# A graph layer with linear attention and an expert network: the flag's work among the first edge groups, chunks of 5 and 3 node tiles, the experts' first products in another bank ring

## The chip, the cores and the metric

The kernel runs on one core of a Trainium2 chip as one launch. The metric is the device time of that launch in microseconds (us), lower is better. In this text PE is TensorE, PEld its weight loads, DVE VectorE, ACT ScalarE, POOL GpSimd and SP SyncE; the last issues DMAs.

## The reference

There are 6250 nodes of 256 features and 106250 edges, sorted by their destination, with 64 edge features each. All numbers are float32.

```python
xn = _layernorm(x)
# graph part: one message per edge, summed over the edges of a destination
msgs = silu(concat([xn[src], edge_attr], -1) @ W + b)
gnn  = layernorm(segment_sum(msgs, dst, 6250)) * gamma + beta
# linear attention over all nodes, 8 heads of 64
q, k, v = split(xn @ Wqkv.T);  k, v = inst_norm(k), inst_norm(v)   # per head
mix  = (q @ (k.T @ v) / 6250) @ Wout.T + bout
x = x + gnn + mix
# expert part: each node goes to one of 32 experts (256 -> 64 -> 256)
xf  = _layernorm(x);  idx = argmax(xf @ router_w.T + router_b)
out = relu(relu(xf @ W1[idx] + b1[idx]) @ W2[idx] + b2[idx])
x = x + out
```

## The kernel before

**Tiles.** The nodes are 49 tiles of 128 (the last is partial). The edges are 208 groups of 512; a group is gathered in four pieces of 128 edges, 831 gathers in all.

**Stage one** (`stage_one`) runs to the first gather. For a pair j of node tiles it normalizes (ACT), transposes on PE (`turn`, L353), multiplies by the node part of the weight on PE (`project`, L363), adds the bias on DVE and stores to `proj` in DRAM. Statistics of the layer norm (DVE; `shift` and `inv`) are dealt out over the pairs. Between pairs, `columns` (L372 to L379) transposes a table of integers held as floats: `src` behind pair 3, right behind its cast on POOL (L394); the places of destinations, `rel`, at pair 10, after POOL's work on `dst` at pair 6; and first columns of `dst` at the end. From these a chain on DVE (to L456) makes `row_of`. Last comes the flag, one number that says whether the fast selection is valid for these edges: an iota `g_i` on POOL, a chain of `bounds` on DVE (from L460), four reductions over 128x896 numbers (L465, L473), a sum over rows by PE (`pflag`, L482) and a copy to `unlike`.

**Edge loop** (from L1562, `for g in range(NG)`). The order of instructions on each engine is that of the program. One turn g issues, in this order: the gathers of group g+3 on POOL (L1432; the tile `gat` has 6 buffers), four products `h` on PE (L1571), the add of `h` and `gat` on DVE (L1573), a selection matrix `s1` on DVE (L1579), the transpose of the edge features of group g+1 (PE L1448, ACT copy L1452), the silu on ACT (L1589), the load of edge features four groups ahead on ACT's DMA queue (L1417), and `work.step`, which lets a planner add other work. Every second turn follows `level2` (PE `sum`, L1553) and `level1` (PE `po`, L1526, ACT copy L1535), which sum the messages of two groups by selection matrices. `po` is the last reader of a `gat` buffer.

**The planner.** `work.step` gives 2.7 us of PE and 3.8 us of DVE a turn to generators in a fixed order, each of which states what its step costs. They are: `attention()` (load and turn the weights, L497 to L523; then batches of two node tiles: `kv`, L540 to L570; then the matrix); `finish()` with one `chunk` per entry of `CHUNKS`; `clears()` (SP stores of zeros); and the expert work. `chunk` mixes, takes moments (DVE), makes `inv2`, normalizes into `wide`, transposes on PE (`pt`, L784, ACT copy `xfT`, L786), makes the router's products (`lg`, L772) for two tiles at a time, then picks the expert (`hot`), and ranks tokens by expert (`prank`, L839, DVE chain with `logit`, L851). The tokens of a round are then sent to rows sorted by expert in DRAM (`send`, POOL, L1051) and read back in blocks by SP (`xb`, L1066), whose weights follow on SP's queue (L1168, L1171, L1217). The first round takes 28 tiles.

**Experts.** `layers` works on quads of blocks: transposes (`pt`, L1088, DVE copy L1094), first products `phid` (L1100), relu on ACT (`hid`, L1110), second products `py` (L1124, L1135), relu on ACT into `xb` (L1144), a store (L1146). Accumulator memory is handed out in rings by tag: "h" one buffer of two banks, "t", "sum" and "kv" two banks each. `phid`, `py`, `kv`, `lg` and `prank` share "kv"; `po` and all transposes share "t". After the last edge group the rest of the work drains ("draining", "late"), and `collect` and `dense` finish the nodes.

Of the kernel before, what the change touches and what calls it, by code (L numbers as in the profile page):

```python
# [8 lines left out]
F32 = mybir.dt.float32  # L9
# [6 lines left out]
PSUM = bass.MemoryType.PSUM  # L16
# [12 lines left out]
GE = P * KE  # L29
KS = 2  # L30
SPAN = P // (KE * KS)
CHUNKS = (6, 6, 6, 5, 5, 5, 5, 4, 3, 2, 2)
CH = max(CHUNKS)
FIRST = (2, 4, 6, 10, 13, 14)
AB = 2
KV = 4
HB = 64
BB = 2
# [24 lines left out]
def kernel(  # L63
# [187 lines left out]
    mix = const.tile([P, DC, D], F32, name="mix")  # L251


    def stage_one(early, pre_ps):
        def bank(tag, shape, name, bufs=2):
            return pre_ps.tile(shape, F32, tag=tag, name=name, bufs=bufs)

# [130 lines left out]
        for j in range(NP + 1):  # L388
            if j < NP:
                turn(j)  # L390
            if j + 1 < NP:
                normalize(j + 1)
            if j == 3:
                nc.gpsimd.tensor_copy(src_f, src_r)  # L394
                columns(lambda b: src_f[:, b, :], src_T)
            if j == 6:
                nc.gpsimd.tensor_copy(dst_f, dst_r)
                nc.gpsimd.tensor_sub(rel, dst_f, dst_f[:, :, 0:1].to_broadcast([P, EB, P]))
            if j == 10:
                columns(lambda b: rel[:, b, :], rel_T)  # L400
            if j >= 1:
                pp = project(j - 1)
            if j >= 1:
                add(j - 1, pp)
            go_on(j)
# [48 lines left out]
                row_of[q, :], row_of[q, :], h_f[q, :], by_sum[q, 0, k, :], op0=ALU.mult, op1=ALU.add  # L454
            )
        nc.vector.scalar_tensor_tensor(row_of, row_of, r_f, starts, op0=ALU.add, op1=ALU.subtract)  # L456

        g_i = early.tile([P, EB], I32, name="g_i")
        nc.gpsimd.iota(g_i, pattern=[[P, EB]], base=0, channel_multiplier=1)
        nc.vector.tensor_scalar(g_i, g_i, (KE * KS).bit_length() - 1, None, op0=ALU.logical_shift_right)  # L460
        g_f = early.tile([P, EB], F32, name="g_f")
        nc.vector.tensor_copy(g_f, g_i)
        low, high = bounds(g_f, [P, EB], "tb")
        bad = early.tile([P, EB], F32, name="bad")
        nc.vector.tensor_reduce(bad, rel, axis=AX.X, op=ALU.max)  # L465
        nc.vector.tensor_scalar(bad, bad, float(SPAN), None, op0=ALU.is_ge)
        for source, op, limit, test in (
            (rel, ALU.min, None, ALU.is_lt),
            (dst_f, ALU.max, high, ALU.is_ge),
            (dst_f, ALU.min, low, ALU.is_lt),  # L470
        ):
            some = early.tile([P, EB], F32, name="some", bufs=2)
            nc.vector.tensor_reduce(some, source, axis=AX.X, op=op)  # L473
            if limit is None:
                nc.vector.tensor_scalar(some, some, 0.0, None, op0=test)
            else:
                nc.vector.tensor_tensor(some, some, limit, op=test)
            nc.vector.tensor_add(bad, bad, some)
        bad1 = early.tile([P, 1], F32, name="bad1")
        nc.vector.tensor_reduce(bad1, bad, axis=AX.X, op=ALU.add)  # L480
        pb = bank("o", [1, 1], "pflag", 3)
        nc.tensor.matmul(pb, bad1, ones[:, 0:1], start=True, stop=True)  # L482
        nc.vector.tensor_copy(unlike, pb)

# [131 lines left out]
    class Nodes:  # L616
# [114 lines left out]
        def chunk(self, t0, t1):  # L731
# [4 lines left out]
            def behind(stage):  # L736
                return before is None or self.at[before] >= stage
# [11 lines left out]
                moments(mv2, t - t0, X[:, t, :])  # L749
                yield pe, dve + 0.6, int(t == t1 - 1)  # L750
            self.at[t0] = 1
            while not behind(2):
                yield 0.0, 0.0, 1
            inv2 = inv_std(mv2, m, LN_EPS, "l2")
            on_act = self.in_order and self.work.draining
            if on_act:
# [2 lines left out]
                    shift[:, :m], mv2[:, :m, 0], -1.0, inv2[:, :m], op0=ALU.mult, op1=ALU.mult  # L759
                )  # L760
            yield 0.0, 1.9, 1
            logit = self.pool.tile([P, CH, NE], F32, name="logit", bufs=2)
            pairs = [list(range(t, min(t + 2, t1))) for t in range(t0, t1, 2)]
            turned = {}
            for i in range(len(pairs) + 2):
                pe = dve = 0.0
                if i >= 2:
                    lg = self.bank("kv", [P, 2, NE], "lg")
                    for k, t in enumerate(pairs[i - 2]):
                        xfT = turned.pop(t)  # L770
                        for c in range(DC):
                            nc.tensor.matmul(  # L772
                                lg[:, k, :], xfT[:, c, :], rw_t[:, c, :], start=(c == 0), stop=(c == DC - 1)
                            )
                    n, q = len(pairs[i - 2]), pairs[i - 2][0] - t0
                    nc.vector.tensor_add(
                        logit[:, q : q + n, :], lg[:, :n, :], rb[:, None, :].to_broadcast([P, n, NE])
                    )
                    pe, dve = pe + 0.5, dve + 0.3
                if 1 <= i <= len(pairs):  # L780
                    for t in pairs[i - 1]:
                        pt = self.bank("t", [P, DC, P], "pt")
                        for c in range(DC):
                            nc.tensor.transpose(pt[:, c, :], wide[:, t, c * P : (c + 1) * P], ident)  # L784
                        turned[t] = self.pool.tile([P, DC, P], F32, name="xfT", bufs=2)
                        nc.scalar.copy(turned[t], pt)  # L786
                    pe += 0.5
                if i < len(pairs):
                    for t in pairs[i]:
                        k = t - t0  # L790
                        if on_act:
                            nc.scalar.activation(
                                wide[:, t, :],
                                X[:, t, :],
                                AF.Identity,
                                bias=shift[:, k : k + 1],
                                scale=inv2[:, k : k + 1],
                            )
                            continue
                        nc.vector.tensor_scalar(  # L800
                            wide[:, t, :],
                            X[:, t, :],
                            mv2[:, k, 0:1],
                            inv2[:, k : k + 1],
                            op0=ALU.subtract,
                            op1=ALU.mult,
                        )
                        dve += 0.4
                yield pe, dve, 1
# [268 lines left out]
        def layers(self, pool, r, b0, xb, w1_of, w2_of, b1_of, one_of):  # L1078
# [14 lines left out]
            else:  # L1093
                nc.vector.tensor_copy(xbT, pt)  # L1094
            yield 0.6, 0.0 if late else 0.7, 1, 1.0
            ph = self.bank("kv", [P, QB // BB, HB], "phid")
            for j in pairs:
                for c in range(DC):
                    for i in range(BB):
# [284 lines left out]
    def ordered(arm):  # L1384
        with ExitStack() as edge_scope:
# [6 lines left out]
            ]  # L1392
            nodes = Nodes(node, rounds, True)
            work = nodes.work
            with tc.tile_pool(name="early", bufs=1) as early, tc.tile_pool(name="pre_ps", bufs=2, space=PSUM) as pre_ps:
                stage_one(early, pre_ps)
            psum = arm.enter_context(tc.tile_pool(name="psum", bufs=2, space=PSUM))

            def bank(tag, shape, name, bufs=2):
                return psum.tile(shape, F32, tag=tag, name=name, bufs=bufs)  # L1400

            nodes.bank = bank
            nodes.load_biases()
            opens = {t: min(g for g in range(NQ) if window(g)[0] <= t <= window(g)[1]) for t in range(NT)}
            closes = {t: max(g for g in range(NQ) if window(g)[0] <= t <= window(g)[1]) for t in range(NT)}
# [60 lines left out]
                closed.append((t0, t1))  # L1466

            attn_scope = ExitStack()
            attn = attn_scope.enter_context(tc.tile_pool(name="attn", bufs=1))
            moe_scope = ExitStack()  # L1470
            closed = []

            def attention():
                w = {}
                yield from weights(attn, bank, w)
                batches = []
# [345 lines left out]
```

## Time and profile before

| | |
|---|---|
| four runs | 1360.34, 1362.83, 1364.42, 1365.96 us; median 1363.62 |
| profiled execution | 1361.14 us, span 1359.3, mean granted clock 0.918 |
| busy | PE 1120.7 us (82%), DVE 823.3 (61%), ACT 564.5 (42%), POOL 943.7 (69%) |
| gathers | first 85.30, last 1236.86 us; 831 of 965 ns |
| DMA | 227.60 MB, mean 167 GB/s |

A row of a timeline reads: start in us, duration, engine, line, operation, out<-in, how many, and in brackets the idle time of that engine before it with what ended it. Instructions of one kind in a row are drawn together. "issue" means that the engine waited for nothing that the profile shows. The wait table gives the waiting instruction, what it waited for, the sum in us, how often, and the longest.

### The profile page before, as it was taken

The numbers are of one execution on the slowest core, as the hardware profiler recorded it, in microseconds if no ns is written. First come the engines' busy times: TensorE is split into PE (matmuls) and PEld (weight loads), VectorE is DVE, ScalarE is ACT, GpSimd is POOL, SyncE is SP. The second block draws the span as 40 slices with busy tenths as digits, with TensorE's granted clock in tenths as the row PEclk, the third lists the DMA queues.
The fourth block names the chain that finished last, engine by engine and source line by source line (L and its number), as shares of the span: only waits on it lengthen the run. The fifth ranks groups of instructions, "written<-read, shape, count | busy, mean of one in ns | idle before, by whom it ended". The sixth has DMA issues, their size and how long they took to land. (4 is left out here: it accounts for less than half of the span.)

```text
span 1359.3 us, 24393 instructions
## 1 busy us (share of the span) xinstructions
PE 1120.7 (82%) x8301; PEld 671.9 (49%) x8301; DVE 823.3 (61%) x2107; ACT 564.5 (42%) x1046; POOL 943.7 (69%) x1046
## 2 busy tenths in 40 slices
PE   5948999988888998878978886648878888987796
PEld 4834545444444544445654554325545555553453
DVE  7864767766666777567886777424545555554621
ACT  3725555544545554433333332113434444342342
POOL 3656777777777777777777777775775577573671
PEclk8977999999999999989998998667889999997698
DMA  8349544444444454584444445557887688562494
GB/s 264 116 128 373 142 130 133 132 128 129 132 127 131 130 133 127 144 261 133 129 132 130 127 132 152 166 162 207 237 236 220 193 234 231 172 194 70 143 307 131
DMA packets 243794, 227.60 MB, mean 167 GB/s; under 512 B 130920, under 2 KB 213836, under 8 KB 243660
## 3 DMA queue, kind: packets, MB, share of 16 engines
q0 software_dynamic: 44384, 121.18, 30.6%
q1 hardware_dynamic: 91096, 77.41, 17.8%
q10 hardware_dynamic: 108180, 27.34, 8.9%
q8 instruction: 69, 1.13, 0.3%
q14 instruction: 65, 0.53, 0.1%
HBM read 180.14 MB, written 45.70 MB: 166 GB/s over the span
## 5 line engine op out<-in xcount | busy, mean ns | idle before, releaser
L1432 POOL DMA_INDIRECT gat<-proj,src_T x831 | 802.0, 965 | 304.2 <-issue 246.9
L1573 DVE TENSOR_TENSOR gat<-h,gat 128x1024 f32<-128x1024 f32 x208 | 254.2, 1222 | 270.7 <-PE h L1571 138.3
L1589 ACT ACTIVATE gat<-gat 128x1024 f32<-128x1024 f32 x208 | 219.9, 1057 | 226.2 <-DVE gat L1573 209.4
L1571 PE MATMUL h<-ge,eT 64*128 64x256 f32 x1664 | 249.2, 420 | 44.7 <-DVE gat L1573 43.5
L1571 PEld LDWEIGHTS h<-ge,eT 64*128 64x128 f32 x1664 | 154.6, 196 | 136.0 <-issue 65.7
L1553 PE MATMUL sum<-part,s 128*128 128x256 f32 x400 | 124.0, 436 | 71.5 <-DVE s L1542 70.7
L540 PE MATMUL kv<-kv_w,wide 128*128 128x512 f32 x392 | 180.2, 602 | 2.2 <-DVE kv_w L518 2.2
L1452 ACT COPY eT<-pt 128x256 f32<-128x256 f32 x208 | 77.0, 370 | 201.2 <-PE pt L1448 191.6
L1553 PEld LDWEIGHTS sum<-part,s 128*128 128x128 f32 x400 | 76.4, 211 | 109.0 <-DVE s L1542 95.6
L1526 PE MATMUL po<-gat,s 128*32 128x256 f32 x1664 | 122.9, 417 | 0.0
L1535 ACT COPY part<-po 128x256 f32<-128x256 f32 x104 | 38.7, 372 | 195.2 <-PE po L1526 178.1
L540 PEld LDWEIGHTS kv<-kv_w,wide 128*128 128x128 f32 x392 | 71.8, 194 | 73.8 <-issue 70.4
L1448 PE MATMUL pt<-ident,ea 128*128 128x128 f32 x416 | 92.9, 306 | 5.1 <-ACT xfT L786 4.7
L547 DVE TENSOR_REDUCE var<-sq 128x16 f32<-128x1024 f32 x49 | 59.7, 1219 | 52.9 <-ACT sq L546 52.9
L1448 PEld LDWEIGHTS pt<-ident,ea 128*128 128x128 f32 x416 | 42.5, 143 | 77.2 <-issue 68.8
L1526 PEld LDWEIGHTS po<-gat,s 128*32 128x32 f32 x1664 | 46.0, 116 | 61.0 <-issue 35.1
L1051 POOL DMA_INDIRECT xso<-wide,slot x47 | 47.3, 1005 | 36.4 <-DVE slot L965 26.4
L1094 DVE COPY xbT<-pt 128x512 f32<-128x512 f32 x39 | 26.8, 687 | 64.0 <-PE pt L1088 63.9
L1579 DVE TENSOR_TENSOR s<-rel_T,ramp 128x128 f32<-128x128 f32 x208 | 58.9, 283 | 0.0
L720 PE MATMUL pres<-mix,wide 128*128 128x256 f32 x196 | 53.3, 408 | 5.1 <-DVE X L721 3.5
L543 ACT COPY kv<-kv 128x512 f32<-128x512 f32 x98 | 53.0, 577 | 3.5 <-PE kv L540 2.9
L347 POOL TENSOR_TENSOR X<-X,bo 128x256 f32<-128x256 f32 x49 | 34.7, 729 | 27.3 <-ACT xn L344 23.0
(298 smaller groups left out, 1426.9 us busy)
## 6 DMA issues: line engine op xcount, KB each, us to landing
ea<-in_edge_attr_dram ACTq DMA_DIRECT2D x203, 128.0 KB
gat<-proj,src_T POOLq DMA_INDIRECT x831
xso<-zero SPq DMA_DIRECT2D x51, 256.0 KB
xb<-xso SPq DMA_DIRECT2D x51, 256.0 KB
yso<-xb SPq DMA_DIRECT2D x51, 256.0 KB
proj<-pr SPq DMA_DIRECT2D x24, 256.0 KB
out_dram<-X SPq DMA_DIRECT2D x22, 256.0 KB
w1t<-in_L_ffn_W_dram SPq DMA_DIRECT2D x76, 64.0 KB
```

What stands on the lines that cost most here:

```text
L540: nc.tensor.matmul(b, xnT(t0 + j, c), kv_w[:, c, s * F : (s + 1) * F], start=(c == 0), stop=(c == DC - 1))
L547: nc.vector.tensor_reduce(var[:, j * 2 * HEADS : (j + 1) * 2 * HEADS], sq, axis=AX.X, op=ALU.add)
L720: nc.tensor.matmul(p, xnT(t, c), mix[:, c, :], start=(c == 0), stop=(c == DC - 1))
L1432: nc.gpsimd.indirect_dma_start(out=gat[:n, k % 2, k // 2, :], out_offset=None, in_=proj[:], in_offset=bass.IndirectOffsetOnAxis(ap=src_T[: ...
L1448: nc.tensor.transpose(pt[:, j, :], ea[:, 2 * j : 2 * j + 2, :].rearrange("p k d -> p (k d)"), ident)
L1452: nc.scalar.copy(eT, pt)
L1526: nc.tensor.matmul(po[k * wide_k : (k + 1) * wide_k, :], s1[:, k, :], msg[:, k % 2, k // 2, :], start=(g == here[0]), stop=(g == here[-1]) ...
L1553: nc.tensor.matmul(sums[t], s2[:, (t - lo) * P : (t - lo + 1) * P], part, start=(q == opens[t]), stop=(q == closes[t]),)
L1571: nc.tensor.matmul(h[:, s, j, :], eTs[g][half, j, :], ge[half, :], start=True, stop=True)
L1573: nc.vector.tensor_add(gats[g], h, gats[g])
L1579: nc.vector.tensor_tensor(s1s[g], rel_T[:, at, None].to_broadcast([P, KE, SPAN * KS]), ramp[:, None, r0 : r0 + SPAN * KS].to_broadcast([P, ...
L1589: nc.scalar.activation(gats[g], gats[g], AF.Silu)
```

## The change

It has five parts. (1) `CHUNKS` becomes twelve entries of at most 5, the first round now 5, 5, 5, 5, 5, 3. (2) Up to three tiles (`TG`) go through the router's transposes and products at a time. (3) A chunk may take `inv2` once the chunk before is past its own, and waits for it only afterwards. (4) In stage one the src columns go from pair 3 to 7 with their cast at 4, the dst work from 6 to 9, the rel columns from 10 to 13; and `stage_one` becomes a generator that ends at `row_of`, whose rest, the flag, is handed out by `attention()` in steps of 3.8 us of DVE, ahead of the attention's weights; the tiles of stage one are released only then, and those of the attention opened after that. (5) `phid` takes its accumulator from "t" instead of "kv", except while draining.

```diff
@@ -29,9 +29,10 @@
 GE = P * KE
 KS = 2
 SPAN = P // (KE * KS)
-CHUNKS = (6, 6, 6, 5, 5, 5, 5, 4, 3, 2, 2)
+CHUNKS = (5, 5, 5, 5, 5, 3, 5, 5, 4, 3, 2, 2)
 CH = max(CHUNKS)
 FIRST = (2, 4, 6, 10, 13, 14)
+TG = 3
 AB = 2
 KV = 4
 HB = 64
@@ -251,7 +252,9 @@
     mix = const.tile([P, DC, D], F32, name="mix")
 
 
-    def stage_one(early, pre_ps):
+    def stage_one(early, pre_ps, later_bank):
+
+
         def bank(tag, shape, name, bufs=2):
             return pre_ps.tile(shape, F32, tag=tag, name=name, bufs=bufs)
 
@@ -390,13 +393,14 @@
                 turn(j)
             if j + 1 < NP:
                 normalize(j + 1)
-            if j == 3:
+            if j == 4:
                 nc.gpsimd.tensor_copy(src_f, src_r)
+            if j == 7:
                 columns(lambda b: src_f[:, b, :], src_T)
-            if j == 6:
+            if j == 9:
                 nc.gpsimd.tensor_copy(dst_f, dst_r)
                 nc.gpsimd.tensor_sub(rel, dst_f, dst_f[:, :, 0:1].to_broadcast([P, EB, P]))
-            if j == 10:
+            if j == 13:
                 columns(lambda b: rel[:, b, :], rel_T)
             if j >= 1:
                 pp = project(j - 1)
@@ -454,13 +458,14 @@
                 row_of[q, :], row_of[q, :], h_f[q, :], by_sum[q, 0, k, :], op0=ALU.mult, op1=ALU.add
             )
         nc.vector.scalar_tensor_tensor(row_of, row_of, r_f, starts, op0=ALU.add, op1=ALU.subtract)
-
+        yield
         g_i = early.tile([P, EB], I32, name="g_i")
         nc.gpsimd.iota(g_i, pattern=[[P, EB]], base=0, channel_multiplier=1)
         nc.vector.tensor_scalar(g_i, g_i, (KE * KS).bit_length() - 1, None, op0=ALU.logical_shift_right)
         g_f = early.tile([P, EB], F32, name="g_f")
         nc.vector.tensor_copy(g_f, g_i)
         low, high = bounds(g_f, [P, EB], "tb")
+        yield
         bad = early.tile([P, EB], F32, name="bad")
         nc.vector.tensor_reduce(bad, rel, axis=AX.X, op=ALU.max)
         nc.vector.tensor_scalar(bad, bad, float(SPAN), None, op0=ALU.is_ge)
@@ -469,6 +474,8 @@
             (dst_f, ALU.max, high, ALU.is_ge),
             (dst_f, ALU.min, low, ALU.is_lt),
         ):
+            if limit is high:
+                yield
             some = early.tile([P, EB], F32, name="some", bufs=2)
             nc.vector.tensor_reduce(some, source, axis=AX.X, op=op)
             if limit is None:
@@ -478,7 +485,8 @@
             nc.vector.tensor_add(bad, bad, some)
         bad1 = early.tile([P, 1], F32, name="bad1")
         nc.vector.tensor_reduce(bad1, bad, axis=AX.X, op=ALU.add)
-        pb = bank("o", [1, 1], "pflag", 3)
+        yield
+        pb = later_bank("kv", [1, 1], "pflag")
         nc.tensor.matmul(pb, bad1, ones[:, 0:1], start=True, stop=True)
         nc.vector.tensor_copy(unlike, pb)
 
@@ -749,7 +757,7 @@
                 moments(mv2, t - t0, X[:, t, :])
                 yield pe, dve + 0.6, int(t == t1 - 1)
             self.at[t0] = 1
-            while not behind(2):
+            while not behind(1.5):
                 yield 0.0, 0.0, 1
             inv2 = inv_std(mv2, m, LN_EPS, "l2")
             on_act = self.in_order and self.work.draining
@@ -759,13 +767,18 @@
                     shift[:, :m], mv2[:, :m, 0], -1.0, inv2[:, :m], op0=ALU.mult, op1=ALU.mult
                 )
             yield 0.0, 1.9, 1
+            while not behind(2):
+                yield 0.0, 0.0, 1
+            self.at[t0] = 1.5
             logit = self.pool.tile([P, CH, NE], F32, name="logit", bufs=2)
-            pairs = [list(range(t, min(t + 2, t1))) for t in range(t0, t1, 2)]
+            parts = -(-m // TG)
+            cuts = [t0 + m * i // parts for i in range(parts + 1)]
+            pairs = [list(range(a, b)) for a, b in zip(cuts, cuts[1:])]
             turned = {}
             for i in range(len(pairs) + 2):
                 pe = dve = 0.0
                 if i >= 2:
-                    lg = self.bank("kv", [P, 2, NE], "lg")
+                    lg = self.bank("kv", [P, TG, NE], "lg")
                     for k, t in enumerate(pairs[i - 2]):
                         xfT = turned.pop(t)
                         for c in range(DC):
@@ -776,15 +789,15 @@
                     nc.vector.tensor_add(
                         logit[:, q : q + n, :], lg[:, :n, :], rb[:, None, :].to_broadcast([P, n, NE])
                     )
-                    pe, dve = pe + 0.5, dve + 0.3
+                    pe, dve = pe + 0.25 * n, dve + 0.3
                 if 1 <= i <= len(pairs):
                     for t in pairs[i - 1]:
                         pt = self.bank("t", [P, DC, P], "pt")
                         for c in range(DC):
                             nc.tensor.transpose(pt[:, c, :], wide[:, t, c * P : (c + 1) * P], ident)
-                        turned[t] = self.pool.tile([P, DC, P], F32, name="xfT", bufs=2)
+                        turned[t] = self.pool.tile([P, DC, P], F32, name="xfT", bufs=TG)
                         nc.scalar.copy(turned[t], pt)
-                    pe += 0.5
+                        pe += 0.25
                 if i < len(pairs):
                     for t in pairs[i]:
                         k = t - t0
@@ -1093,7 +1106,8 @@
             else:
                 nc.vector.tensor_copy(xbT, pt)
             yield 0.6, 0.0 if late else 0.7, 1, 1.0
-            ph = self.bank("kv", [P, QB // BB, HB], "phid")
+
+            ph = self.bank("kv" if late else "t", [P, QB // BB, HB], "phid")
             for j in pairs:
                 for c in range(DC):
                     for i in range(BB):
@@ -1392,14 +1406,17 @@
             ]
             nodes = Nodes(node, rounds, True)
             work = nodes.work
-            with tc.tile_pool(name="early", bufs=1) as early, tc.tile_pool(name="pre_ps", bufs=2, space=PSUM) as pre_ps:
-                stage_one(early, pre_ps)
-            psum = arm.enter_context(tc.tile_pool(name="psum", bufs=2, space=PSUM))
 
             def bank(tag, shape, name, bufs=2):
                 return psum.tile(shape, F32, tag=tag, name=name, bufs=bufs)
 
             nodes.bank = bank
+            early_scope = ExitStack()
+            early = early_scope.enter_context(tc.tile_pool(name="early", bufs=1))
+            with tc.tile_pool(name="pre_ps", bufs=2, space=PSUM) as pre_ps:
+                first_stage = stage_one(early, pre_ps, bank)
+                next(first_stage)
+            psum = arm.enter_context(tc.tile_pool(name="psum", bufs=2, space=PSUM))
             nodes.load_biases()
             opens = {t: min(g for g in range(NQ) if window(g)[0] <= t <= window(g)[1]) for t in range(NT)}
             closes = {t: max(g for g in range(NQ) if window(g)[0] <= t <= window(g)[1]) for t in range(NT)}
@@ -1466,11 +1483,14 @@
                 closed.append((t0, t1))
 
             attn_scope = ExitStack()
-            attn = attn_scope.enter_context(tc.tile_pool(name="attn", bufs=1))
             moe_scope = ExitStack()
             closed = []
 
             def attention():
+                for _ in first_stage:
+                    yield 0.0, 3.8, 0
+                early_scope.close()
+                attn = attn_scope.enter_context(tc.tile_pool(name="attn", bufs=1))
                 w = {}
                 yield from weights(attn, bank, w)
                 batches = []
```

## The prediction

> **What bounds the kernel now.** The busy row first, then the costliest groups.
>
> ```profile
> PE 1120.7 (82%) x8301; PEld 671.9 (49%) x8301; DVE 823.3 (61%) x2107; ACT 564.5 (42%) x1046; POOL 943.7 (69%) x1046
> ...
> L1432 POOL DMA_INDIRECT gat<-proj,src_T x831 | 802.0, 965 | 304.2 <-issue 246.9
> ```
>
> PE is busiest, but most of the span is paced by POOL. POOL's timeline has gathers back to back from 85.30 to 1237.85 us, one each 0.953 + 0.30 = 1.257 us, 5.03 us a group; 831 make 1044.6 of those 1152.6 us. So the loop can lose time only where a gather starts late, and gain only there or at its two ends. These are the first two late places, and two of a long series:
>
> ```profile
> 85.30 1.14 POOL L1432 DMA_INDIRECT gat<-proj,src_T  x1 [8.30 <-DMA b_sb<-in_L_ffn_b_dram]
> ...
> 122.42 0.95 POOL L1432 DMA_INDIRECT gat<-proj,src_T  x1 [6.24 <-ACT kv L543]
> ...
> 925.68 0.95 POOL L1432 DMA_INDIRECT gat<-proj,src_T  x1 [4.47 <-issue]
> ...
> 1010.12 0.95 POOL L1432 DMA_INDIRECT gat<-proj,src_T  x1 [2.43 <-issue]
> ```
>
> The bracket is the idle time before. Between 123 and 925 us no gather is late at all. Net of the usual 0.30, the gathers at 925.68, 936.23 and 950.77 lose 8.8 us, and eleven between 1008 and 1184 lose 27.6. "issue" hides the releaser: a gather reuses the buffer of the group six back, free when PE's po (L1526) has read it, so I read PE and ACT there. PE's timeline:
>
> ```profile
> 20.39 0.93 PE L353 MATMUL pt<-ident,xn 128*128 128x128 f32 x4
> 24.85 1.75 PE L378 MATMUL pt<-ident,src_r 128*128 128x128 f32 x7 [3.53 <-POOL src_r L394]
> 26.39 3.62 PE L363 MATMUL pp<-gw,wide 128*128 128x256 f32 x8
> ...
> 98.01 0.19 PE L482 MATMUL pflag<-ones,bad 128*1 128x1 f32 x2 [17.89 <-DVE bad L480]
> ...
> 99.65 2.08 PE L1571 MATMUL h<-ge,eT 64*128 64x256 f32 x8 [0.18 <-ACT eT L1452]
> ...
> 116.75 4.25 PE L540 MATMUL kv<-kv_w,wide 128*128 128x512 f32 x6 [1.47 <-DVE kv_w L518]
> 120.94 1.07 PE L1526 MATMUL po<-gat,s 128*32 128x256 f32 x16
> ```
>
> Stage one waits 3.53 us for POOL's cast and then runs slow; the first edge group waits until 99.65 behind the flag. PE's waits from 1000 to 1184 us (line, releaser: us, times, longest):
>
> ```profile
> PE phid L1100 <- ACT xb L1144: 14.1, 15, 2.6
> PE py L1124 <- DVE logit L851: 5.1, 2, 3.1
> ```
>
> ACT's timeline:
>
> ```profile
> 907.96 0.37 ACT L1535 COPY part<-po 128x256 f32<-128x256 f32 x1 [15.41 <-DMA w1t<-in_L_ffn_W_dram]
> ```
>
> Here ACT stood 15.41 us: its queue's edge load (L1417, 907.54) was held while SP's load of expert tokens (L1066) waited until 902.61 for POOL's sends.
>
> **Part by part.** The sum is made against the profiled execution: 1361.14 us (span 1359.3), 2.48 under the median 1363.62 of four runs.
>
> *1. Stage one: -5.4.* The order of the changed kernel puts the src columns at pair 7, three pairs after their cast at 4, so the 3.53 goes. The first projection after it took 3.62 where the later ones take 1.89, the next transposes and projection lost 0.46 more: 2.19 of slow clock. Against it, DVE's shift for the third group of tiles is ready only at 27.59, and PE, no longer held by the cast, waits for it some 1.3. That is -4.4. The rel columns at pair 13 instead of 10 spare the 1.00 that PE waited at 47.9. The rest is PE-bound at 2.17 us a pair with the same instructions. Bounds: 0 (all of it comes back as waits for shift) and -6.3. The first gather, S, starts near 79.9 instead of 85.3.
>
> *2. Start of the loop: +8.8.* Nothing of the flag is removed; it is moved among the first groups, and each queue it passes counts. On POOL the iota of g_i now stands behind 16 gathers: S + 16 x 1.257 = S+20.1. DVE waits for it just after the add of group 0, and everything on DVE queues behind: bounds and threshold 4.0 (88.29 to 92.29), the two rel reduces 2.6 (to 94.89): the add of group 1 comes at S+27.0, not S+12. Then the dst reduces 3.1 (94.89 to 98.0) and group 1's own 1.5: bad1 at S+31.5, pflag on PE S+31.7. po(0) is behind it, done S+33.9: the gathers of group 6, due at S + 24 x 1.257 = S+30.2, stall 4.0 (5.94 before). On SP the raw load waits for pflag, as it now takes over the early tiles' space: issued S+32.1 where before it was 98.35 = S+13.0. It took 6.4 us to land, its transposes 5.1 (105.63 to 110.7), and from there to the end of the first kv 10.25 (120.94), all ahead of po(1) in PE's order: S+38.5, S+43.6, S+53.9, po(1) done S+55.6, and group 8's gathers at S+56.0. Before, they were at 132.5 = S+47.2. So +8.8. Lowest: all of it is hidden and the old 5.94 goes, -5.9. Highest: the raw load takes half as long again beside running gathers, +12. I take the worked value, since every wait in it stands in the instruction order. The zeroing stores (32 of 256 KB) shift with it and find no gather due.
>
> PE's rows here are slow ones: h 2.08 against 1.14 later, kv x6 4.25 where x8 takes 3.60 later, at a granted clock of 0.63 from 100 to 122 us. I keep the slow rows, since PE's work stays in pieces with gaps.
> [...]
>
> *3. ACT held behind SP: -6.* With the attention one group shorter and rounds cut at 5-tile chunks, the sends begin after 562 gathers, not 582, and end some 1.5 groups after the xb step rather than 2.5. The held edge load of ACT comes about one group later against them. A group in this stretch takes some 10 us, so most of the 8.8 goes: -6, between 0 and -8.8.
>
> *4. Expert stretch: -15.* phid moves from the bank ring that it shares with py ("kv") to that of the transposes ("t"); the 14.1 us of phid's waits for ACT's xb go. In the new ring it waits for hid's eviction two steps back, which by the rows ends 0.7 to 0.8 us before it is needed: a wait W becomes max(0, W - 1.5), and the long ones (2.6) leave 1.2 in sum. Two groups take 12.2 us on PE here, 10.66 without the waits, against POOL's 10.06: so PE remains the bound by 0.6 and not all 27.6 can go. -14.1 + 1.2, + 2 (below), - 4 since experts start 5 groups earlier (pt of the first quad at group 147, not 152) and fewer groups carry a full load: -15. The 5.1 for the logit stay. Bounds: -6 (the waits go half) and -27.6.
>
> *5. Chunks of five and three, three tiles routed at once: 0,* but for the 2 above. Three transposes in a two-buffer ring: the third waits for ACT's copy, behind a silu of 1.06, some 1.7 us, in 9 steps. Before 925 POOL hides it (no gather late there for 800 us); without that cover it would be 9 x 1.7 = 15. One or two of the 9 fall in the PE-bound part: 2. The statistics step 1.5 only lets DVE start earlier. *Tail: 0,* same instructions after the last gather, one rank batch earlier, one quad moved; ±3.
>
> Sum: -5.4 + 8.8 - 6 - 15 = -17.6: own time 1343.5, on the median 1346.0.
>
> **Rivals.** *Forecast,* .54: terms as above, with their middle spreads 1336 to 1356. *The waits come back,* .12: hid in the "t" ring, beside po and the ea transposes, makes phid wait for ACT as long as xb did. For: ACT is one engine, and hid, xb and silu queue on it. Against: ACT is 42% busy. Then part 4 is -3: -5.6, 1358. *All stalls vanish,* .06: start hidden (-5.9), the 27.6 and 8.8 gone: -5.4 - 5.9 - 8.8 - 27.6 = -47.7, 1316; with half of part 2's price 1331. *No change,* .10: waits come back and part 3 gives nothing: +0.4, 1364; this is also the case in which the bank move does not do what it says. *Slower,* .18: the held edge load. ACT's queue is in order, so its edge load stands where the program put it; if the sends, now among more routing work, end late, it comes earlier against them, not later. Two groups earlier cost 2 x 10 us on top of the lost 6: -17.6 + 6 + 20 = +8.4, 1372. It decides from 1.2 groups (12 us). For: the 15.41 us are one wait with nothing behind it to fill in. Against: the order shows the sends earlier.
>
> **How the numbers follow.** About 0.3% (4 us) is what a measurement can tell. Faster .54 + .12 + .06 = .72, same .10, slower .18. The range goes from 1331 (leaving most of the .06) to 1370 (leaving some .14 of the slower). The likeliest case alone: 1336 to 1356.
>
> **What would show it.** First gather at 79 to 81 and no wait before the src columns; DVE idle before L460 of about 10 us; the two late gathers at groups 6 and 8 with 4 and 11 us; no phid <- xb in PE's waits, and gathers of 1000 to 1180 late by under 15 in all; ACT's longest wait near the sends under 10. I am wrong if group 8 starts before S+47 or after S+60, if phid waits for hid by over 8 us in all, or if a gather before 900 is late.

## The result, and the profile after

The changed kernel takes 1365.54 us (median of 42 runs, 1353.47 to 1373.14), the kernel before 1363.66 (63 runs): ratio 1.0014, 95% interval 1.0002 to 1.0025. That is no change by the bound of the prediction, where 1346.0 was forecast. The profiled execution took 1369.97 us, 4.4 above its median, that of before 1361.14, 2.5 below its own; so the two traces differ by 8.9 us of span where the medians differ by 1.9. In three series (the experiments name them) the kernel before itself took 1834 to 1857 us, every kernel profiled there had a granted clock near 0.80 and gathers late by over 100 us in all before 650 us, and no time of those is used.

The page of the changed kernel, busy row and first group:

```profile
PE 1127.0 (82%) x8305; PEld 675.2 (49%) x8305; DVE 829.1 (61%) x2135; ACT 565.0 (41%) x1046; POOL 938.3 (69%) x1046
...
L1449 POOL DMA_INDIRECT gat<-proj,src_T x831 | 797.9, 960 | 313.5 <-issue 267.9
```

The line numbers used here have moved by 13 to 20 (gathers L1449, `h` L1591, `po` L1546, `select` L1562, `sum` L1573, `phid` L1114, `pt` L797, `xfT` L799). The late gathers of POOL's timeline, those of the start and the two largest of a new series:

```profile
86.45 1.25 POOL L1449 DMA_INDIRECT gat<-proj,src_T  x1 [8.48 <-DMA ea<-in_edge_attr_dram]
...
120.09 0.94 POOL L1449 DMA_INDIRECT gat<-proj,src_T  x1 [3.47 <-issue]
...
141.12 0.94 POOL L1449 DMA_INDIRECT gat<-proj,src_T  x1 [11.33 <-issue]
...
715.05 0.94 POOL L1449 DMA_INDIRECT gat<-proj,src_T  x1 [4.58 <-issue]
...
742.04 0.94 POOL L1449 DMA_INDIRECT gat<-proj,src_T  x1 [4.86 <-issue]
```

Before, one gather was late between 123 and 925 us, by 0.5; now eleven are between 700 and 812. Put together from both timelines (late means the idle time before a gather beyond the usual 0.30 us; the tail runs from the start of the last gather to the end of the span):

| us | forecast | before | after | difference |
|---|---|---|---|---|
| first gather at | -5.4 | 85.30 | 86.45 | +1.2 |
| gather 32, after the first | +8.8 | 47.2 | 54.7 | +7.5 |
| late, routing (650 to 836) | 0 | 0.5 | 21.1 | +20.6 |
| late, sends (900 to 1000) | -6 | 8.8 | 4.6 | -4.2 |
| late, experts (after 1000) | -15 | 27.6 | 12.5 | -15.1 |
| tail | 0 | 122.4 | 124.8 | +2.4 |
| a gather's own 965, now 960 ns, x 831 | 0 | | | -4.2 |

The differences sum to +8.2, of the +8.9 in the spans. The two gains that were forecast inside the loop came; the loss came in a stretch that the forecast had at nothing. PE's waits there, 690 to 840 us:

```profile
PE sum L1573 <- DVE s L1562: 16.7, 8, 5.3
PE h L1591 <- DVE gat L1593: 7.9, 7, 2.1
PE pt L797 <- ACT xfT L799: 6.8, 5, 2.6
PE prank L852 <- DVE hot L833: 3.0, 4, 2.2
```

and the engines in its middle (columns: span of the stretch, busy time of PE, PEld, DVE, ACT, POOL with instructions, granted clock, DMA share, GB/s):

```profile
740.00:780.00 40.00, 29.38 (x193) 17.75 (x194) 26.71 (x77) 12.57 (x23) 26.05 (x27) 0.79 0.39 106
```

PE is busy 73% of it and POOL 65%: nobody is full. PE, ACT and DVE wait for one another in turn, and POOL for all of them.

### The profile page after: what moved, and what is told of

Its sections match the earlier page's. It is cut to its first block, busy times and chain, and to the rows that moved or that the text cites. A ratio compares the mean times of both kernels' runs of the same rounds, so it can differ in the third digit from the quotient of the medians.

```text
span 1368.2 us, 24440 instructions
## 1 busy us (share of the span) xinstructions
PE 1127.0 (82%) x8305; PEld 675.2 (49%) x8305; DVE 829.1 (61%) x2135; ACT 565.0 (41%) x1046; POOL 938.3 (69%) x1046
## 3 DMA queue, kind: packets, MB, share of 16 engines
q8 instruction: 69, 1.13, 0.4%
## 5 line engine op out<-in xcount | busy, mean ns | idle before, releaser
L1449 POOL DMA_INDIRECT gat<-proj,src_T x831 | 797.9, 960 | 313.5 <-issue 267.9
L1591 PE MATMUL h<-ge,eT 64*128 64x256 f32 x1664 | 250.8, 422 | 60.4 <-DVE gat L1593 60.1
L1591 PEld LDWEIGHTS h<-ge,eT 64*128 64x128 f32 x1664 | 155.1, 197 | 154.1 <-issue 91.6
L1573 PE MATMUL sum<-part,s 128*128 128x256 f32 x400 | 126.9, 444 | 77.1 <-DVE s L1562 76.6
L1573 PEld LDWEIGHTS sum<-part,s 128*128 128x128 f32 x400 | 78.1, 214 | 114.3 <-DVE s L1562 98.2
L1546 PE MATMUL po<-gat,s 128*32 128x256 f32 x1664 | 125.9, 426 | 1.3 <-ACT eT L1469 0.7
L1465 PE MATMUL pt<-ident,ea 128*128 128x128 f32 x416 | 93.4, 307 | 11.5 <-DMA ea<-in_edge_attr_dram 5.7
L1546 PEld LDWEIGHTS po<-gat,s 128*32 128x32 f32 x1664 | 46.7, 118 | 64.4 <-issue 33.8
L1158 ACT ACTIVATE xb<-py 128x256 f32<-128x256 f32 x102 | 34.5, 378 | 48.2 <-PE py L1149 31.0
```

Of the source, the lines that this page charges most:

```text
L1449: nc.gpsimd.indirect_dma_start(out=gat[:n, k % 2, k // 2, :], out_offset=None, in_=proj[:], in_offset=bass.IndirectOffsetOnAxis(ap=src_T[: ...
L1465: nc.tensor.transpose(pt[:, j, :], ea[:, 2 * j : 2 * j + 2, :].rearrange("p k d -> p (k d)"), ident)
L1546: nc.tensor.matmul(po[k * wide_k : (k + 1) * wide_k, :], s1[:, k, :], msg[:, k % 2, k // 2, :], start=(g == here[0]), stop=(g == here[-1]) ...
L1573: nc.tensor.matmul(sums[t], s2[:, (t - lo) * P : (t - lo + 1) * P], part, start=(q == opens[t]), stop=(q == closes[t]),)
L1591: nc.tensor.matmul(h[:, s, j, :], eTs[g][half, j, :], ge[half, :], start=True, stop=True)
```

## The experiments

Each kernel was timed beside the kernel before on the same chip; the ratio is to that.

**The bank alone.** The kernel before, and in `layers`:

```diff
-            ph = self.bank("kv", [P, QB // BB, HB], "phid")
+            ph = self.bank("kv" if late else "t", [P, QB // BB, HB], "phid")
```

> The kernel before with one line of the change: phid takes its accumulator from the ring "t" instead of "kv". Theory (the shared ring cost the expert stretch its late gathers, and the bank is what gave 16.6 us of them back): phid no longer waits for ACT's xb, the late gathers between 1000 and 1190 us fall from 27.6 to 13 or less, the time to about 1350 (-10 to -16). Rival (PE's total work decides, the gathers only came on time after 1000 because experts started five groups earlier): the waits turn up elsewhere in the same stretch, late gathers stay over 22, time 1360 to 1364.

Measured: 1345.87 us against 1362.64, ratio 0.9867 (0.9845 to 0.9888). Late gathers after 1000 us fall from 27.6 to 12.2, and phid's wait for ACT's xb is gone from PE's waits of 1000 to 1184 us, whose first row is now the wait for the logit that was second before:

```profile
PE py L1124 <- DVE logit L851: 5.2, 2, 3.1
PE sum L1553 <- DVE s L1542: 3.0, 1, 3.0
```

Theory held. So one line gives by itself nearly the 17.6 us that were forecast for the whole change, and the rest of the change as it stands took them away again.

**Two tiles at a time.** The changed kernel with

```diff
-TG = 3
+TG = 2
```

> The changed kernel with tiles routed two at a time (TG 2, so a chunk of 5 goes as 1, 2, 2). Theory A (packing): sends start after 582 gathers here too, so the late gathers between 700 and 836 us fall to under 6, time about 1350. Theory B (three transposes): PE's waits for ACT's xfT, 6.8 us in that stretch, go, and 12 or more of the 21 us with them; time about 1350 here while the kernel with only inv2 put back stays at 1362 or more. Theory C: as there, time the same within 4.

Measured: 1344.88 us against 1362.64, ratio 0.9868 (0.9843 to 0.9893). Late gathers in the routing stretch: 2.7 us instead of 21.1; the tail: 119.3 instead of 124.8. Among PE's waits of 690 to 840 us none of the router's transposes (L797) for xfT is left:

```profile
PE sum L1573 <- DVE s L1562: 14.4, 8, 3.6
PE h L1591 <- DVE gat L1593: 7.3, 7, 2.7
PE pt L797 <- DVE wide L813: 3.0, 2, 2.3
```

Theories A and B both forecast this, so only the next kernels tell them apart.

**The earlier inv2 undone.** The changed kernel with

```diff
-            while not behind(1.5):
+            while not behind(2):
```

> The changed kernel with one part undone: a chunk takes inv2 only once the chunk before has been through its logits (stage 2 instead of 1.5). Theory A (routing packed into fewer groups by the earlier inv2 puts more DVE and PE work on a group than POOL's 5.03 us hide): the 21 us of late gathers between 700 and 836 us go to under 6, sends start after 582 gathers again, time about 1350 (-15). Theory B (three transposes in a ring of two make PE wait for ACT, whatever the chunks' order): late gathers there stay at 12 to 21, time within 6 us of the changed kernel's. Theory C (PE's load only moves: what is not paid here is paid with the experts): late gathers go here and come back after 1000 us, time the same within 4.

Measured: 1353.71 us, ratio 0.9936 (0.9911 to 0.9962). Its sends, too, start after 582 gathers, as with two tiles at a time. But 11.5 us of late gathers stay in the routing stretch, with 5.6 us of PE's waits for xfT, and the tail is 126.7. From the first `prank` to the sixth the changed kernel takes 23 turns, this one 28, the one with two tiles 27. So these two spread the routing over nearly the same number of groups and differ in the size of a step: theory A (packing) explains 10 of the 21 us and not the rest. Theory C is out: after 1000 us 11.8 us are late (12.5 in the changed kernel), and the time fell.

**Three at a time without the wait in the ring of two.** The changed kernel with

```diff
-                    for t in pairs[i - 1]:
-                        pt = self.bank("t", [P, DC, P], "pt")
+                    for k, t in enumerate(pairs[i - 1]):
+                        pt = self.bank("kv" if k == 2 else "t", [P, DC, P], "pt")
```

> The changed kernel, packed as it is (sends after 562 gathers), with the third tile's transposes from the ring "kv". The changed kernel works a chunk of 5 tiles off in 4 turns, 1.25 tiles a turn; a tile costs PE about 1.9 us (pres 0.93, pt 0.44, lg 0.49), a turn without tiles 2.5, waits about 0.9: 5.8 us a group against POOL's 5.03. Theory A (this density): without the waits for xfT (1.1 to 2.6 us a chunk) a group still takes 5.5, so the late gathers of 690 to 836 us go from 21 to 12 to 15 only, time about 1358. Theory B (the ring wait itself): they go to under 8, time about 1350.

Measured: 1363.85 us against 1365.15, ratio 1.0000 (0.9983 to 1.0017). The waits for xfT are gone, and PE's time goes into the next ones:

```profile
PE sum L1573 <- DVE s L1562: 17.2, 8, 5.3
PE h L1591 <- DVE gat L1593: 6.8, 6, 2.2
PE prank L852 <- DVE hot L833: 3.1, 4, 2.3
PE pres L728 <- DVE logit L864: 2.6, 1, 2.6
```

Late gathers in the routing stretch: 16.1 us, more than theory A's 12 to 15. So theory B falls as the cause by itself: 5 of 21 us.

**Three at a time, one more turn a chunk.** The changed kernel with one more `yield 0.0, 0.0, 1` ahead of `self.at[t0] = 2`.

> The changed kernel, three tiles at a time from the ring of two as it is, but a chunk gives away one more turn after its logits, so the sends start after 586 gathers. Theory A (density: 5 tiles in 5 turns instead of 4, so a turn costs PE 0.5 us less): late gathers of 690 to 836 us under 10 though the waits for xfT stay, time 1347 to 1354. Theory B (the third transpose's wait): 15 or more of the 21 us stay, time about 1360.

Measured: 1359.79 us against 1362.88, ratio 0.9972 (0.9944 to 0.9999); 13.0 us late in the routing stretch, 6.3 us of waits for xfT, tail 129.6. From the first `prank` to the sixth it takes 28 turns, so it is spread as far as the kernel with the earlier inv2 undone, and is late by about as much. The time is theory B's, the late gathers lie between the two theories: two ways of spreading the steps leave 11.5 and 13.0 us, and only smaller steps take them to 3.

**The flag whole again.** The changed kernel with the flag run out at the end of stage one and the columns at their old places:

```diff
-            if j == 4:
+            if j == 3:
                 nc.gpsimd.tensor_copy(src_f, src_r)
-            if j == 7:
...
-                first_stage = stage_one(early, pre_ps, bank)
-                next(first_stage)
+                first_stage = stage_one(early, pre_ps, own_bank)
+                for _ in first_stage:
+                    pass
+            early_scope.close()
```

> The changed kernel with its fourth part undone: the flag whole at the end of stage one, src columns at pair 3, dst at 6, rel at 10, as before. Theory (handing the flag out cost 7.5 us at gather 32 and won nothing in stage one): first gather within 1 us of 85.3 to 86.5, gather 32 about 47 us after the first instead of 54.7, and since POOL paces the loop up to 700 us, all of it reaches the end: time -7 to -9, about 1357. Rival (the later stretches are bound by PE and take up the lead): time within 3 us of the changed kernel's, late gathers after 690 us larger by 5 or more.

Measured: 1361.45 us, ratio 0.9990 (0.9968 to 1.0011). Gather 32 stands 48.3 us after the first (54.7 in the changed kernel), but only some 4 of these 6.4 us arrive at the end (1361.45 against 1365.54, of different series), fewer than theory's 7 to 9; the rival is out, as the late gathers after 690 us did not grow. The gathers take 967 ns here, not 960, which is 6 us over all of them. The routing stretch is late by 19.2 all the same, so the start is not its cause. With two tiles at a time as well:

> The changed kernel with two parts undone: two tiles at a time, and the flag whole at the end of stage one with the columns at their old places. What is left of the change is the bank of phid, chunks of 5 and 3 and the earlier inv2. Theory (the parts add up): 1344.9 of the kernel with two tiles, less the 4 us that undoing the start was worth in the changed kernel: 1338 to 1342. Rival (what the start wins is taken up by later stretches, or by the gathers, which take 967 ns instead of 960 when the flag is whole: 831 x 7 ns = 5.8 us): 1343 to 1346.

Measured: 1341.99 us against 1362.88, ratio 0.9858 (0.9823 to 0.9894). Gather 32 at 48.5, no late gather in the routing stretch, gathers of 966 ns. This is the upper edge of the theory's range, 2.9 us under the kernel with two tiles; but the intervals of the two ratios overlap.

**The iota ahead of the gathers.** The kernel with two tiles at a time, and

```diff
-        yield
         g_i = early.tile([P, EB], I32, name="g_i")
         nc.gpsimd.iota(g_i, pattern=[[P, EB]], base=0, channel_multiplier=1)
+        yield
```

> The kernel with two tiles at a time, and the iota of g_i ahead of the gathers on POOL instead of behind 16 of them. Theory (that iota's place on POOL's queue is what makes the start late: DVE, pflag, the raw load and po wait for it one behind the other): DVE goes on behind the add of group 0 without a wait, pflag some 10 us earlier, gather 32 at 44 to 47 us after the first instead of 54.5, time 1336 to 1339. Rival (the flag's DVE work and the raw load's 6.4 us are what is late, the iota only the first of them): gather 32 at 51 us or later, time 1342 or more.

Measured: 1334.65 us (1330.15 to 1335.84) against 1362.88, ratio 0.9793 (0.9761 to 0.9825): the fastest kernel here, 2.1% under the kernel before. DVE's first step of the flag, in the changed kernel and here:

```profile
106.78 0.17 DVE L464 TENSOR_SCALAR g_i<-g_i 128x7 int32<-128x7 int32 x1 [11.88 <-POOL g_i L463]
```
```profile
94.17 0.16 DVE L464 TENSOR_SCALAR g_i<-g_i 128x7 int32<-128x7 int32 x1
```

The wait of 11.88 us is gone, pflag runs at 105.23 instead of 118.09, and gather 32 stands 40.45 us after the first, which is 32 x 1.257 + 0.2: no gather of the start is late any more. Theory held, and the gain was larger than it said. Here the flag handed out is free at the gathers, once what it waits for is not itself behind them.

**Stage one.** Two kernels: the kernel before with the columns moved alone, and the one with the iota first with statistics one pair earlier:

```diff
-            begin, end = 0 if i < 4 else firsts[i - 1][0] // 2 - 2, t0 // 2 - 3
+            ahead = int(i in (3, 4))
+            begin, end = 0 if i < 4 else firsts[i - 1][0] // 2 - 2 - ahead, t0 // 2 - 3 - ahead
```

> The kernel before with only the columns moved (src to pair 7 with its cast at 4, dst to 9, rel to 13). Prediction's step 1: first gather 5 us earlier, time about 1358. Theory now (DVE's chain for the shift of the 10 and 13 tiles sets stage one, not the casts): no wait of PE before the src columns, but waits for ACT's xn of 2 to 3 us at about 30 and 46 us, first gather at 84 to 86.5, time 1362 to 1365.

> The kernel with two tiles at a time and the iota first, with the statistics of the groups of 10 and 13 tiles dealt out one pair earlier, so that their chains on DVE stand one or two adds earlier (0.67 us each). Theory (DVE's chain for shift sets the end of stage one): PE's waits at about 30 and 46 us (2.45 and 2.96 in the changed kernel) shrink by 0.7 to 1.4 each, first gather 1.3 to 2.5 us earlier than 84.2 to 86.5, time 1332 to 1334. Rival (something else, a load or POOL's casts, is behind the chain): the waits stay within 0.4, time as without it, 1334.7.

Their times (1834.87 us beside 1833.61 for the kernel before, and 1869.08 beside 1856.64) are not used, being of the series named under the result; the first 80 us of their traces can be compared with the other kernels (the columns alone: PE's waits 2.23 and 3.17 us at 30.05 and 45.77, first gather 86.08, as theory had it). With the statistics earlier the shift of 13 tiles comes at 40.15 instead of 45.13:

```profile
40.15 0.17 DVE L323 SCALAR_TENSOR_TENSOR shift<-st_m,inv 128x13 f32<-128x13 f32 x1
```

The wait at 46 us is gone, that at 30 us is 2.20 and so stays, and the first gather is at 81.29, where the other kernels with moved columns have 84.2 to 86.5. So DVE's chain sets stage one, at its second wait; what that is worth in time was not measured.

**Runs whose times are not used.** The changed kernel with phid back in "kv":

> The changed kernel with phid back in the ring "kv". Theory (the bank's gain is whole inside the change and the other parts ate it): late gathers after 1000 us back from 12.5 to 25 or more, PE's wait of phid for ACT's xb back at 10 us or more, time 1378 to 1383. Rival (experts starting five groups earlier make room enough): late gathers after 1000 us under 18, time 1365 to 1371.

It took 1860.77 us beside 1856.64 for the kernel before. What the bank is worth inside the changed kernel is therefore not shown by itself; that the bank takes the late gathers after 1000 us from 27.6 to 12 rests on the kernel before with and without it. In the other two series four kernels above ran for the first time, beside 1833.61 and 1835.58 us for the kernel before. Third tile from "kv", 1850.69 and 1848.73 us:

> The changed kernel, three tiles at a time and packed as it is (sends after 562 gathers), but the third tile's transposes take their accumulator from the ring "kv". Theory B (the third transpose's wait for ACT in the ring of two is what the routing stretch loses): PE's waits for xfT there go from 6.8 us to under 2, the late gathers of 690 to 836 us from 21 to under 8, time about 1350. Theory A (too much of a chunk's work in each group, whatever the ring): the xfT waits go but the late gathers stay at 15 or more, time 1360 to 1366.

> The changed kernel, three tiles at a time and packed as it is (sends after 562 gathers), but the third tile's transposes take their accumulator from the ring "kv". Theory B (the third transpose's wait for ACT in the ring of two is what the routing stretch loses): PE's waits for xfT there go from 6.8 us to under 2, the late gathers of 690 to 836 us from 21 to under 8, time about 1350. Theory A (too much of a chunk's work in each group, whatever the ring): the xfT waits go but the late gathers stay at 15 or more, time 1360 to 1366.

One more turn a chunk, 1870.94 both times:

> The changed kernel, three tiles at a time from the ring of two as it is, but a chunk gives away one more turn after its logits, so the sends start after 586 gathers. Theory A (packing): late gathers of 690 to 836 us under 6, time about 1347. Theory B (third transpose): PE's xfT waits stay at 5 to 7 us and 10 or more of the 21 us of late gathers with them; time about 1355.

> The changed kernel, three tiles at a time from the ring of two as it is, but a chunk gives away one more turn after its logits, so the sends start after 586 gathers. Theory A (packing): late gathers of 690 to 836 us under 6, time about 1347. Theory B (third transpose): PE's xfT waits stay at 5 to 7 us and 10 or more of the 21 us of late gathers with them; time about 1355.

The flag whole with two tiles, 1825.17 and 1834.74:

> The changed kernel with two parts undone: two tiles at a time, and the flag whole at the end of stage one with the columns at their old places. What is left of the change is the bank of phid, chunks of 5 and 3 and the earlier inv2. Theory (the parts add up): 1344.9 of the kernel with two tiles, less the 6 to 7 us that gather 32 is earlier: 1337 to 1340. Rival (what the start wins is taken up by later stretches, or by the gathers, which take 967 ns instead of 960 when the flag is whole: 831 x 7 ns = 5.8 us): 1343 to 1346.

> The changed kernel with two parts undone: two tiles at a time, and the flag whole at the end of stage one with the columns at their old places. What is left of the change is the bank of phid, chunks of 5 and 3 and the earlier inv2. Theory (the parts add up): 1344.9 of the kernel with two tiles, less the 6 to 7 us that gather 32 is earlier: 1337 to 1340. Rival (what the start wins is taken up by later stretches, or by the gathers, which take 967 ns instead of 960 when the flag is whole: 831 x 7 ns = 5.8 us): 1343 to 1346.

The iota first, 1844.12:

> The kernel with two tiles at a time, and the iota of g_i ahead of the gathers on POOL instead of behind 16 of them. Theory (that iota's place on POOL's queue is what makes the start late: DVE, pflag, the raw load and po wait for it one behind the other): DVE goes on behind the add of group 0 without a wait, pflag some 10 us earlier, gather 32 at 44 to 47 us after the first instead of 54.5, time 1336 to 1339. Rival (the flag's DVE work and the raw load's 6.4 us are what is late, the iota only the first of them): gather 32 at 51 us or later, time 1342 or more.

The order of these times is not that of the later runs of the same kernels (with one more turn a chunk 2% above the kernel before, where later it was 0.3% below), and nothing is concluded from it.

## Why the prediction was wrong

**The step that failed is the fifth: "0, but for the 2 above", with "Before 925 POOL hides it".** The cover was read off a stretch in which the kernel before worked off 22 tiles in 26 turns (counted between the `prank` of its first and fifth chunk), 0.85 a turn; the changed kernel works off 23 in 23 (first to sixth `prank`), and the ten between its second and fourth `prank` in 8, which is 1.25. A warning could have been worked out from rows that were there. A tile costs PE 1.9 us (pres 0.93, `pt` 0.44, `lg` 0.49), a turn without tiles 2.5, the waits 0.9. At 0.85 that is 5.0 us, just POOL's 5.03, so there was no cover to spare; at 1.25 it is 5.8. By this estimate the 23 turns lose some 6 us (5.3 us a turn on average); they took 6.0 each, so density alone does not give the whole loss. The prediction did hold a price for lost cover, 15 us, and the sends 20 gathers earlier were even read in the order, but counted as a gain for the experts and not as more work in each group before them. The loss was 20.6 us in the loop and 2.4 in the tail. That three at a time is the cause is shown (two at a time: 2.7 us late, and 1344.88 us). It has two halves: with three at a time spread over 28 turns 11.5 and 13.0 us stay late, so the packing is worth 8 to 10; from there to 2.7 it is the size of the step, 9 to 10, of which the wait in the ring is a part (5 us went with it in the packed kernel). Another part is PE's wait for DVE's selection, from the first `prank` to the sixth; with one more turn a chunk (28 turns, 689.2 to 838.5 us) and with two at a time (27 turns, 688.7 to 818.0 us):

```profile
PE sum L1574 <- DVE s L1563: 16.5, 10, 3.6
```
```profile
PE sum L1573 <- DVE s L1562: 7.6, 6, 1.9
```

All of PE's waits make 29.4 us there against 18.8, and `sum` takes near 2 us instead of 1.1 in 5 of 14 places against 2 of 13, in the changed kernel in 6 of 12. So larger steps go with longer waits for DVE and with more slow rows behind them; which operation of DVE makes those waits longer, and how the 9 to 10 us divide, stays open.

**Step 1 was mis-sized by 6.6 us** (forecast -5.4, measured +1.2). The wait for POOL's cast went, as said, but PE then waits for ACT's xn, that is DVE's shift, 2.45 us at 30.54 (1.3 foreseen) and 2.96 at 46.04 (none foreseen). The last link of the second chain started at 46.02 before and at 45.13 after: stage one already stood on it, and the columns had been running in its shadow. Single traces with the same stage one differ in the first gather by 1 to 2 us (85.30 before, 84.24 with the bank alone; 84.2 to 86.5 with the columns moved), so the sign of the +1.2 means little; the 5.4 did not come in any of them.

```profile
30.54 0.93 PE L356 MATMUL pt<-ident,xn 128*128 128x128 f32 x4 [2.45 <-ACT xn L347]
...
46.04 1.08 PE L356 MATMUL pt<-ident,xn 128*128 128x128 f32 x4 [2.96 <-ACT xn L347]
```

The second chain on DVE, and POOL beside it, in the changed kernel:

```profile
42.73 0.17 DVE L182 SCALAR_TENSOR_TENSOR ln_h<-ln_h 128x13 f32<-128x13 f32 x1
42.94 1.54 DVE L184 SCALAR_TENSOR_TENSOR ln_z<-ln_h,ln_guess 128x13 f32<-128x13 f32 x1
44.51 0.17 DVE L186 TENSOR_TENSOR ln_sq<-ln_z 128x13 f32<-128x13 f32 x1
...
45.13 0.17 DVE L323 SCALAR_TENSOR_TENSOR shift<-st_m,inv 128x13 f32<-128x13 f32 x1
```
```profile
41.74 0.93 POOL L401 CAST dst_r<-dst_r 128x896 f32<-128x896 int32 x1
42.75 1.70 POOL L402 TENSOR_TENSOR rel<-dst_r 128x896 f32<-128x896 f32 x1
```

And the second of these DVE operations before, where POOL is idle at that time:

```profile
45.18 0.17 DVE L183 SCALAR_TENSOR_TENSOR ln_z<-ln_h,ln_guess 128x13 f32<-128x13 f32 x1
```

The same small operation takes 0.17 us alone and 1.54 beside POOL's subtraction, which ends at 44.45, 0.03 us ahead of it. Before, the end of the dst work and six additions into X that POOL had put off behind it (40.47 to 44.70) lay beside the same chain, and seven of its operations took 0.59 to 0.74 us, two 0.16 and 0.17; so the chain had slow operations with the dst work in the old place and in the new, beside POOL's work both times. Why operations of DVE are longer there, and why not all of them, is not shown.

**Steps 2, 3 and 4 held.** The start: 4.0 and 11.7 us were forecast for the gathers of groups 6 and 8, 3.17 and 11.03 came (3.47 and 11.33 less 0.30), by the waits named; g_i stood behind 16 gathers, pflag at S+31.6 (forecast S+31.7), the raw load at S+32.0 (S+32.1), gather 32 at S+54.7 (S+56.0). The sends: -4.2 for -6; ACT's longest wait there is 10.1 us (15.4 before), so the rival of an edge load held longer is not seen. The experts: -15.1 for -15, and -16.8 of time for the bank alone. That the size fits is partly luck: the bank alone takes 15.4 us off the late gathers, where its own two terms made -12.9, and the 4 us put down to an earlier start of the experts are not seen (12.5 us late in the changed kernel, 12.2 with the bank alone). The rival "the waits come back" is out: 12.5 us stay late, not 24.6, and no row of phid waits for hid. The slow rows kept in step 2 were right: the granted clock from the first gather to gather 32 fell further, from 0.67 to 0.55.

The prediction's own sign of being wrong, a gather late before 900 us, came. The rival *No change* has the number that was measured but not the mechanism: it let the waits of phid come back, and they did not. Three slips of the prediction change nothing in this: the 27.6 us are of ten gathers, not eleven; one gather between 123 and 925 us was late, by 0.5; and the 1331 of *All stalls vanish* takes part 2's price whole, where half of it gives about 1326.

The sum was thus not wrong where the change meant to gain but in what its fifth part cost; with two tiles at a time the changed kernel takes 1344.9, against a forecast of 1346.0 that had the start wrong by 6.6 the other way and gave nothing for the gathers' 4.2. That agreement is partly luck.

## What to carry to other kernels

Cover read off a trace belongs to the density of work in that trace: when a change packs the same work into fewer turns, divide the work anew by the turns and compare it, and its largest single step, with the pace of the engine that hides it, before writing a zero. A chain handed out among other work costs what its first wait costs, so anything it needs from a queue that is always full goes ahead of that queue (here one iota of 0.14 us was worth 10 us). And when a wait is taken away, look for the next chain that ends within the same microsecond, because that one sets the time.

## What the hardware showed that was not expected

A gather takes 965 to 968 ns in the four kernels with the flag whole, and 960 in the five with it handed out as in the change; with the iota first it is 966 again. Over 831 gathers that is 4 to 6 us. The cause was not looked for.

PE's rows after long waits take nearly twice as long: in the routing stretch of the changed kernel, from the first `prank` to the sixth, `sum` takes 1.03 or 1.13 us in half of its places and 2.08 behind each of the three waits of 2.9 to 3.4 us, as in this row:

```profile
723.54 2.08 PE L1573 MATMUL sum<-part,s 128*128 128x256 f32 x4 [3.38 <-DVE s L1562]
725.55 1.94 PE L1546 MATMUL po<-gat,s 128*32 128x256 f32 x16
```

This wait of 3.4 us costs about 3 more, for `po` and `h` behind it are slow as well (1.94 and 2.07 against 1.07 and 1.14). The granted clock was 0.51 over these three (723.54 to 729.42 us) and 1.00 over the fast ones from 712.60 to 715.60. The rows behind the wait of 2.90 us are as slow, and twice slow rows of `sum` (2.08 and 2.07 us) stand behind waits of only 0.69 and 0.65 in the same stretch, while behind one of 0.61 it takes 1.13; whether shorter waits ahead of those add up is not shown.
